# Seven block products for the r and z gates of a five-layer gated graph network, with two groups in flight, on one Trainium2 core

## The chip, the core and the metric

The kernel runs on one core of one Trainium2 chip. Time is device time in microseconds (us). Before any change it is 2644.72 us (median of 3 runs, 2644.05 to 2645.42). The *granted clock* is the share of TensorE's full clock that the profile records; 1.00 is full speed. The kernels are judged faster or slower when they differ by more than 2%.

Five engines work side by side: TensorE (PE in the profile, its weight loads PEld), VectorE (DVE), ScalarE (ACT), GpSimd (POOL) and SyncE (SP, which here only starts DMAs). The program gives each its own instructions in a fixed order.

## The reference

There are 128 graphs of 64 nodes with 256 features. The first stage runs five layers of message passing with a gated cell. Three other residual stages with a layer norm each follow. Only the first stage changes.

```python
def _gru_cell(m, h, w_ih, w_hh, b_ih, b_hh):
    gi = m @ w_ih.T + b_ih
    gh = h @ w_hh.T + b_hh
    i_r, i_z, i_n = jnp.split(gi, 3, axis=-1)
    h_r, h_z, h_n = jnp.split(gh, 3, axis=-1)
    r = jax.nn.sigmoid(i_r + h_r)
    z = jax.nn.sigmoid(i_z + h_z)
    n = jnp.tanh(i_n + r * h_n)
    return (1.0 - z) * n + z * h
...
for l in range(weight.shape[0]):                    # 5 layers
    m = jnp.einsum('bnd,de->bne', h, weight[l])
    agg = jnp.einsum('bij,bid->bjd', A, m)
    h = _gru_cell(agg, h, w_ih, w_hh, b_ih, b_hh)
...                                                 # then: layer norm, neighbour MLP, tangent-space
...                                                 # support, attention, each with a layer norm
```

## The kernel before

Eight graphs, 512 rows, make a group. There are 16 groups, and three are in flight (`NF = 3` sets of buffers). The program is written as one stream of operations per group. A helper, `Flow`, merges the streams into one order for each engine. It looks a few operations ahead (`AHEAD`) and works with durations written into the program. Everything of a layer lies transposed: 256 features as two tiles `c` of 128 partitions, and 512 rows along the free dimension.

A layer first turns the state into rows (`ps_hr`), then sums over neighbours (`ps_agg`). The message weights are multiplied into the gate weights once, at the start (`wmih`). Names that begin with `p_` or `ps_` are *banks*, the buffers that TensorE writes its results to. `hT` is the state, `x` the input of a group, `x_n` the result of a layer norm, and `junk_d` a scratch tile of the attention. What follows the five layers is called the *late stages*. For each of the two feature tiles:

```python
    AHEAD = {"PE": 24, "DVE": 6, "ACT": 6, "POOL": 4, "SP": 2}
    ...
    NF = 3
    ...
                wmi = wmih[l]
                i_n = 2 * KD + c
                p_r = gate(0, [(whhT, hT), (wmi, agg)], "p_r")      # 4 matmuls of 512 columns
                p_hn = gate(2, [(whhT, hT)], "p_hn")                # 2
                p_in = gate(2, [(wmi, agg)], "p_in")                # 2
                p_z = gate(1, [(whhT, hT), (wmi, agg)], "p_z")      # 4
                ...                                                 # r, n, and h - n on ACT and DVE
                act(512, lambda p=p_z, z=tb, c=c: nc.scalar.activation(
                    z.tile(), p.tile(), AF.Tanh, bias=half_b[:, KD + c:KD + c + 1], scale=0.5), [tb], [p_z, half_b])
                dve(512, lambda d=tc_, z=tb: nc.vector.scalar_tensor_tensor(
                    d.tile(), z.tile(), 1.0, d.tile(), OP.add, OP.mult), [tc_], [tc_, tb])
                dve(512, lambda d=tc_, t=ta, h=hn: nc.vector.scalar_tensor_tensor(
                    h.tile(), d.tile(), 0.5, t.tile(), OP.mult, OP.add), [hn], [tc_, ta])
```

The gate z comes last. So only a tanh and two VectorE steps lie between the last matmul and the new state.

Of the kernel before, what the change touches and what calls it, by code (L numbers as in the profile page):

```python
# [50 lines left out]
class Flow:  # L51
# [8 lines left out]
    AHEAD = {"PE": 24, "DVE": 6, "ACT": 6, "POOL": 4, "SP": 2}  # L60
# [83 lines left out]
def kernel(  # L144
# [28 lines left out]

    nc = tc.nc
# [11 lines left out]
    NF = 3  # L186
# [25 lines left out]
    def pe(n, run, w, r):  # L212
        flow.op("PE", {512: 0.86, 256: 0.46, 257: 0.46, 128: 0.33}.get(n, 0.3), run, w, r)
# [58 lines left out]
    whhT = [fixed([P, 3 * D], f"whhT{k}") for k in range(KD)]  # L272
    wattT = [fixed([P, D], f"wattT{k}") for k in range(KD)]


    wmih = [[fixed([P, 3 * D], f"wmih{l}_{k}") for k in range(KD)] for l in range(L)]
# [6 lines left out]
    vecs = fixed([NC, P], "vecs")  # L283
    nmr = fixed([NBLK, P], "nmr")
# [10 lines left out]
    for src, q, tag in ((w_hh, "sync", "hT"), (w_ih, "scalar", "half"), (att_w, "scalar", "agg")):  # L295
        nf = src.shape[0] // P
        for c in range(0, nf, 2):
            raw = {"hT": unit("hT", S, f"raw_hh{c}", (P, 2, D), 4),
                   "half": unit("ABC"[c // 2], S, f"raw_ih{c}", (P, 2, D)),
                   "agg": unit("agg", S, "raw_att", (P, 2, D), 2)}[tag]  # L300
            flow.op("SP" if q == "sync" else "ACT", 3.0 if q == "sync" else 0.1,
                    lambda raw=raw, src=src, c=c, q=q: getattr(nc, q).dma_start(
                        raw.tile(), src.rearrange("(c p) d -> p c d", p=P)[:, c:c + 2, :]), [raw])
            raw_of[src.tensor.name, c] = raw
    wms = []
    for l in range(L):
        wm = [unit("xn", S, f"wm{l}", (P, KD, D), 2), unit("xn", S, f"wm{l}", (P, KD, D), 2),
              unit("y", S, f"wm{l}", (P, KD, D)), unit("x", S, f"wm{l}", (P, KD, D)),
              unit("y", S - 1, f"wm{l}", (P, KD, D))][l]
        flow.op("ACT", 0.1, lambda wm=wm, l=l: nc.scalar.dma_start(  # L310
            wm.tile(), w_msg[l].rearrange("(k p) e -> p k e", p=P)), [wm])
        wms.append(wm)
# [15 lines left out]
    def turned(src, nf, dsts):  # L328
        for k in range(KD):
            for c0 in range(0, nf, 4):  # L330
                n = min(4, nf - c0)
                ps = bank("ps_w")
                for c in range(c0, c0 + n):
                    raw = raw_of[src.tensor.name, c - c % 2]
                    turn(lambda ps=ps, raw=raw, c=c, c0=c0, k=k: nc.tensor.transpose(
                        ps[:, (c - c0) * P:(c - c0 + 1) * P], raw[:, c % 2, k * P:(k + 1) * P], ident.tile()),
                        [ps], [raw, ident])
                dve(n * P, lambda ps=ps, k=k, c0=c0, n=n: nc.vector.tensor_copy(
                    dsts[k][:, c0 * P:(c0 + n) * P], ps[:, :n * P]), [(dsts[k], c0)], [ps])

    wihT = [unit("hr", S, f"wihT{k}", (P, 3 * D), 2) for k in range(KD)]
    turned(w_hh, 3 * KD, whhT)
    turned(w_ih, 3 * KD, wihT)

    for l in range(L):
        ps = bank("ps_wmT")
        for e in range(KD):
# [4 lines left out]
        wmT = unit("hT" if l % 2 else "agg", S, f"wmT{l}", (P, KD, D), 4 if l % 2 else 2)  # L352
        dve(512, lambda ps=ps, wmT=wmT: nc.vector.tensor_copy(
            wmT.tile(), ps.tile().rearrange("p (e d) -> p e d", d=D)), [wmT], [ps])
        for k in range(KD):
            for j, n in ((0, 2 * D), (2 * D, D)):
                ps = bank("ps_wmih")
                for e in range(KD):
                    pe(n, lambda ps=ps, wmT=wmT, e=e, k=k, j=j, n=n: matmul(
                        ps[:, :n], wmT[:, e, k * P:(k + 1) * P], wihT[e][:, j:j + n], e, KD),  # L360
                        [ps], [wmT, wihT[e]])
                act(n, lambda ps=ps, l=l, k=k, j=j, n=n: nc.scalar.copy(wmih[l][k][:, j:j + n], ps[:, :n]),
                    [(wmih[l][k], j)], [ps])
# [6 lines left out]
    turned(att_w, KD, wattT)  # L370
# [13 lines left out]
    def bih(i):  # L384
        return cols[:, i:i + 1]
# [10 lines left out]
    def group(g):  # L396
# [12 lines left out]
        def rows_T(tag, name, bufs, src):  # L409

            dst = [u(tag, f"{name}{k}", bufs=bufs) for k in range(KD)]
            for k in range(KD):
                ps = bank("ps_T")
                for b in range(NB):
                    turn(lambda ps=ps, b=b, k=k: nc.tensor.transpose(  # L415
                        ps[:, b * P:(b + 1) * P], src[:, b, k * P:(k + 1) * P], ident.tile()), [ps], [(src, b)])
                act(R, lambda ps=ps, k=k: nc.scalar.copy(dst[k].tile(), ps.tile()), [dst[k]], [ps])
            return dst
# [30 lines left out]
        hT = rows_T("hT", "hT", 4, xt)  # L449


        hr = None
        for l in range(L):
            agg = [u("agg", f"agg{l}_{c}", bufs=2) for c in range(KD)]
            for c in range(KD):
                if l:
                    hr = u("hr", f"hr{l}_{c}", (P, NB, P), 2)
                    ps = bank("ps_hr")
                    for b in range(NB):
                        turn(lambda ps=ps, b=b, h=hT[c]: nc.tensor.transpose(  # L460
                            ps[:, b * P:(b + 1) * P], h[:, b * P:(b + 1) * P], ident.tile()), [ps], [hT[c]])
                    act(512, lambda ps=ps, hr=hr: nc.scalar.copy(hr.tile(), tiles_of(ps.tile())), [hr], [ps])
                ps = bank("ps_agg")
                for b in range(NB):
                    def one(ps=ps, b=b, c=c, l=l, hr=hr):
                        h = hr[:, b, :] if l else xt[:, b, c * P:(c + 1) * P]
                        matmul(ps[:, b * P:(b + 1) * P], h, ed[:, b, :], 0, 1)
                    pe(128, one, [ps], [hr if l else xt, ed])
                act(512, lambda ps=ps, a=agg[c]: nc.scalar.copy(a.tile(), ps.tile()), [agg[c]], [ps])  # L469
            hN = [u("hT", f"hT{l}_{c}", bufs=4) for c in range(KD)]  # L470
            for c in range(KD):
                def gate(i, sides, name):
                    ps = bank(name)
                    f = slice((i * KD + c) * P, (i * KD + c + 1) * P)
                    n = len(sides) * KD
                    for a, (w, v) in enumerate(sides):
                        for k in range(KD):
                            pe(512, lambda a=a, k=k, w=w, v=v: matmul(ps.tile(), w[k][:, f], v[k].tile(), a * KD + k, n),
                               [ps], [w[k], v[k]])
                    return ps  # L480

                wmi = wmih[l]
                i_n = 2 * KD + c
                p_r = gate(0, [(whhT, hT), (wmi, agg)], "p_r")
# [272 lines left out]
```

## Time and profile before

| what | before |
|---|---|
| time, median | 2644.72 us |
| TensorE busy | 2563.2 us, 97% |
| VectorE, ScalarE, GpSimd busy | 50%, 35%, 12% |
| second to thirteenth output store | 1727.22 us, 157.0 a group |
| TensorE in that stretch | busy 1719.65 us, granted clock 1.00 |

The **period** is the time of the thirteenth output store less that of the second, divided by 11. It is the time that a group costs in the steady state. The view by windows splits it into TensorE's busy and idle time. Its columns are the window, its length, the busy time (and count) of PE, PEld, DVE, ACT and POOL, the granted clock, the DMA share and GB/s. For the kernel before:

```profile
452.96:2180.18 1727.22, 1719.65 (x5911) 969.18 (x5910) 890.65 (x2175) 630.65 (x1105) 215.32 (x242) 1.00 0.03 8
```

1719.65 of 1727.22: in a period of 157.0 us TensorE is busy for 156.3 and idle for 0.7. The largest wait of TensorE in this stretch, with its total, number and longest, is:

```profile
PE ps_hr L460 <- DVE hT L506: 2.8, 4, 1.0
```

### The profile page before, as it was taken

The page shows a single profiled execution, that of the slowest core. Times are in us where ns is not written, and L with a number is a line of the kernel's source. Part 1 is how long each engine was busy: PE and PEld are TensorE (multiplying, and loading weights), DVE is VectorE, ACT ScalarE, POOL GpSimd, SP SyncE. Part 2 cuts the span into 40 slices and gives each one's busy share as a digit, 9 for nine tenths or more (in the row PEclk, how much of TensorE's full clock was granted, in tenths as well). Part 3 has the DMA queues.
Part 4 walks back from the last instruction along what each step waited for, and adds up shares of the span by engine and source line. Part 5 has one row for each costly group of instructions (what it writes and reads, how often), then busy time and mean ns, then how long its engine had stood idle before and what let it go on. Part 6 is the DMA issues. An engine that isn't in the chain of part 4 may idle for free.

```text
span 2642.7 us, 24329 instructions
## 1 busy us (share of the span) xinstructions
PE 2563.2 (97%) x8770; PEld 1448.5 (55%) x8770; DVE 1312.2 (50%) x3191; ACT 933.4 (35%) x1637; POOL 321.5 (12%) x374
## 2 busy tenths in 40 slices
PE   6999999999999999999999999999999999999974
PEld 4556555464655556565565655546465564655543
DVE  1335455463555535455464555536455463545535
ACT  2334333342433334333343433334333333433321
POOL 1002010100202002020110202011020200202010
PEclk9999999999999999999999999999999999999986
DMA  4000000000000000000000000000000000000000
GB/s 120 3 0 10 9 3 17 0 11 8 3 16 3 16 0 11 9 3 16 3 9 8 11 8 3 17 0 11 8 1 16 1 8 9 1 9 1 8 0 8
DMA packets 30696, 26.24 MB, mean 10 GB/s; under 512 B 9668, under 2 KB 30176, under 8 KB 30576
## 3 DMA queue, kind: packets, MB, share of 16 engines
q1 hardware_dynamic: 26416, 19.67, 2.4%
q10 hardware_dynamic: 3760, 4.46, 0.6%
q8 instruction: 69, 1.13, 0.2%
q0 software_dynamic: 400, 0.57, 0.1%
q14 instruction: 51, 0.42, 0.1%
HBM read 16.30 MB, written 8.39 MB: 9 GB/s over the span
## 4 chain that ended last, share of the span: by engine, by line
PE 89%; DVE 5%; ACT 2%; POOL 1%; DMA 1%; issue 1%; POOLq 0%; DVEq 0%; SPq 0%; ACTq 0%
PE p_r L210 19%; PE p_z L210 19%; PE p_hn L210 10%; PE p_in L210 10%; PE ps_o L210 9%; PE ps_hid L210 8%; PE ps_agg L210 5%; PE ps_a L210 2%; PE ps_hr L460 2%; PE ps_wmih L210 1%; PE ps_T L415 1%; PE ps_att L210 1%; DVE st L424 1%; PE ps_sup L210 1%; POOL rstd L427 1%
## 5 line engine op out<-in xcount | busy, mean ns | idle before, releaser
L210 PE MATMUL p_r<-hT,whhT 128*128 128x512 f32 x640 | 311.8, 593 | 0.0
L210 PE MATMUL p_r<-agg,wmih 128*128 128x512 f32 x640 | 304.6, 593 | 0.9 <-ACT agg L469 0.9
L210 PE MATMUL p_hn<-hT,whhT 128*128 128x512 f32 x640 | 305.1, 592 | 0.0
L210 PE MATMUL p_in<-agg,wmih 128*128 128x512 f32 x640 | 304.9, 592 | 0.0
L210 PE MATMUL p_z<-agg,wmih 128*128 128x512 f32 x640 | 304.8, 593 | 0.0
L210 PE MATMUL p_z<-hT,whhT 128*128 128x512 f32 x640 | 304.4, 592 | 0.0
L495 DVE SCALAR_TENSOR_TENSOR A<-A,B 128x512 f32<-128x512 f32 x160 | 114.4, 715 | 360.0 <-ACT B L493 359.6
L498 ACT ACTIVATE A<-A,cols 128x512 f32<-128x512 f32 x160 | 115.5, 722 | 319.6 <-DVE A L497 319.6
L210 PE MATMUL ps_hid<-aggm,w1s 128*128 128x512 f32 x512 | 223.6, 595 | 0.2 <-ACT aggm L540 0.2
L491 ACT ACTIVATE A<-p_r,half_b 128x512 f32<-128x512 f32 x160 | 109.7, 686 | 313.8 <-PE p_r L210 252.9
L501 ACT ACTIVATE B<-p_z,half_b 128x512 f32<-128x512 f32 x160 | 109.6, 685 | 304.2 <-PE p_z L210 304.1
L426 POOL TENSOR_SCALAR ve<-mv 128x4 f32<-128x4 f32 x64 | 19.0, 297 | 1622.4 <-DVE mv L425 1622.4
L504 DVE SCALAR_TENSOR_TENSOR C<-B,C 128x512 f32<-128x512 f32 x160 | 113.9, 712 | 178.3 <-ACT B L501 175.3
L210 PEld LDWEIGHTS p_r<-agg,wmih 128*128 128x128 f32 x640 | 118.5, 190 | 136.5 <-issue 133.2
L210 PEld LDWEIGHTS p_z<-hT,whhT 128*128 128x128 f32 x640 | 119.6, 190 | 133.9 <-issue 130.6
L210 PEld LDWEIGHTS p_in<-agg,wmih 128*128 128x128 f32 x640 | 119.7, 190 | 133.5 <-issue 130.6
L210 PEld LDWEIGHTS p_hn<-hT,whhT 128*128 128x128 f32 x640 | 119.0, 190 | 132.2 <-issue 124.4
L210 PEld LDWEIGHTS p_z<-agg,wmih 128*128 128x128 f32 x640 | 119.6, 190 | 130.9 <-issue 129.6
L210 PE MATMUL ps_o<-w2s,hid 128*128 128x256 f32 x768 | 182.8, 384 | 5.1 <-DVE hid L587 5.1
L210 PEld LDWEIGHTS ps_o<-w2s,hid 128*128 128x128 f32 x768 | 146.9, 193 | 40.8 <-issue 9.1
L500 DVE TENSOR_TENSOR C<-hT,A 128x512 f32<-128x512 f32 x160 | 118.1, 738 | 97.0 <-ACT A L498 97.0
L210 PEld LDWEIGHTS p_r<-hT,whhT 128*128 128x128 f32 x640 | 112.6, 191 | 95.0 <-issue 91.1
(160 smaller groups left out, 3245.4 us busy)
## 6 DMA issues: line engine op xcount, KB each, us to landing
x<-in_x_dram SPq DMA_DIRECT2D x16, 512.0 KB, 3.9
out_dram<-x_n SPq DMA_DIRECT2D x16, 512.0 KB, 2.9
a_raw<-in_adj_dram SPq DMA_DIRECT2D x32, 64.0 KB, 2.5
wm<-in_L_gnn_weight_dram ACTq DMA_DIRECT2D x5, 256.0 KB, 7.0
w1s<-in_L_gnn_W_dram ACTq DMA_DIRECT2D x1, 1024.0 KB, 11.2
w2s<-in_L_gnn_W_dram ACTq DMA_DIRECT2D x1, 1024.0 KB, 11.2
raw_ih<-in_L_gnn_w_ih_dram ACTq DMA_DIRECT2D x3, 256.0 KB, 5.3
raw_hh<-in_L_gnn_w_hh_dram SPq DMA_DIRECT2D x3, 256.0 KB, 6.8
```

What stands on the lines that cost most here:

```text
L210: nc.tensor.matmul(o, lhsT, rhs, start=(k == 0), stop=(k == nk - 1))
L415: turn(lambda ps=ps, b=b, k=k: nc.tensor.transpose(ps[:, b * P:(b + 1) * P], src[:, b, k * P:(k + 1) * P], ident.tile()), [ps], [(src, b)])
L424: dve(256, lambda b=b: nc.vector.bn_stats(st[:, b, :], y[:, b, :]), [(st, b)], [(y, b)])
L426: pool(0.23, lambda: nc.gpsimd.tensor_scalar(ve.tile(), mv[:, :, 1], LN_EPS, None, OP.add), [ve], [mv])
L427: pool(1.04, lambda: nc.gpsimd.tensor_tensor(rstd.tile(), ve.tile(), m_half, OP.pow), [rstd], [ve])
L460: turn(lambda ps=ps, b=b, h=hT[c]: nc.tensor.transpose(ps[:, b * P:(b + 1) * P], h[:, b * P:(b + 1) * P], ident.tile()), [ps], [hT[c]])
L491: act(512, lambda p=p_r, t=ta, c=c: nc.scalar.activation(t.tile(), p.tile(), AF.Tanh, bias=half_b[:, c:c + 1], scale=0.5), [ta], [p_r, hal ...
L495: dve(512, lambda t=ta, v=tb: nc.vector.scalar_tensor_tensor(t.tile(), t.tile(), 1.0, v.tile(), OP.add, OP.mult), [ta], [ta, tb])
L498: act(512, lambda t=ta, i=i_n: nc.scalar.activation(t.tile(), t.tile(), AF.Tanh, bias=bih(i)), [ta], [ta, cols])
L500: dve(512, lambda d=tc_, h=hc, t=ta: nc.vector.tensor_sub(d.tile(), h.tile(), t.tile()), [tc_], [hc, ta])
L501: act(512, lambda p=p_z, z=tb, c=c: nc.scalar.activation(z.tile(), p.tile(), AF.Tanh, bias=half_b[:, KD + c:KD + c + 1], scale=0.5), [tb], ...
L504: dve(512, lambda d=tc_, z=tb: nc.vector.scalar_tensor_tensor(d.tile(), z.tile(), 1.0, d.tile(), OP.add, OP.mult), [tc_], [tc_, tb])
```

## The change

Gates r and z are a block product. The left factor is the 2 x 2 block matrix of a11, a12 (message and state weights of r) and a21, a22 (those of z). The right factor has the summed message `a` above the state `h`, each cut into row halves 0 and 1. Eight block products give it in the plain way. Strassen's method, in a form with few sums, needs seven. The weight sums s1 to s4 are made once on the chip. Four sums of data (t1 to t4) go to GpSimd in each layer. Five sums of products (`plus`) go to VectorE. TensorE should lose an eighth of its work on r and z. The five weight sets for each layer and the sums take so much on-chip memory that only two groups fit.

```diff
-    AHEAD = {"PE": 24, "DVE": 6, "ACT": 6, "POOL": 4, "SP": 2}
+    AHEAD = {"PE": 32, "DVE": 10, "ACT": 10, "POOL": 4, "SP": 2}
...
-    NF = 3
+    NF = 2
+    HR = R // 2
...
+            for o, x0, x1 in ((s1[l], a21, na22), (s2[l], s1[l], a11[l]), (s3[l], a11[l], a21), (s4[l], a12, s2[l])):
...
+        def product(ps, w, v, first, last, r):
+            for c in range(KD):
+                for k in range(KD):
+                    pe(256, lambda c=c, k=k: nc.tensor.matmul(
+                        ps[:, c * HR:(c + 1) * HR], w[:, k, c * P:(c + 1) * P], v(k), ...
...
+            minus(t1, of(a, 1), of(a, 0), [a])                       # GpSimd
+            minus(t2, of(h, 1), lambda: view(t1), [(h, 1), t1])
+            minus(t3, of(h, 1), of(a, 1), [(h, 1), (a, 1)])
+            minus(t4, lambda: view(t2), of(h, 0), [t2, (h, 0)])
+            ...                                                      # state part of n, as before
+            product(p1, a11[l], k_of(a, 0), True, False, (a, 0))
+            act(512, lambda: nc.scalar.copy(u1.tile(), blocks_of(p1.tile())), [u1], [p1])
+            product(p_in[0], w_in[l], k_of(a, 0), True, True, (a, 0))
+            product(p1, a12, k_of(h, 0), False, True, (h, 0))
+            tanh_half(ur, lambda c: p1[:, c * HR:(c + 1) * HR], 0, p1)   # r, half 0
+            product(pu, s2[l], k_view(t2), True, True, t2)
+            plus(uu, pu, u1)                                         # VectorE
+            product(pv, s3[l], k_view(t3), True, False, t3)
+            plus(uv, pv, uu)
+            product(p_in[1], w_in[l], k_of(a, 1), True, True, (a, 1))
+            product(pv, na22, k_view(t4), False, True, t4)
+            plus(uz, pv, uu)
+            tanh_half(uz, lambda c: uz[:, c, :], 1, uz)              # z, half 0
+            new_state(0, ur, uz)
+            product(pw, s1[l], k_view(t1), True, False, t1)
+            plus(uv, pw, uv)                                         # must read pw ...
+            product(pw, s4[l], k_of(h, 1), False, True, (h, 1))      # ... before this adds to it
+            plus(uu, pw, uu)
+            tanh_half(uu, lambda c: uu[:, c, :], 0, uu)              # r, half 1: the last
+            tanh_half(uv, lambda c: uv[:, c, :], 1, uv)              # z, half 1
+            new_state(1, uu, uv)
```

`new_state` is five VectorE steps of 512 and one tanh in two parts. It ends with the new state of that row half. In the profile of after, `ta` and `tb` are the tiles of t1 to t4, and U, V, Z, R are the gates and their partial sums.

## The prediction

> **What bounds the kernel now.** I read the busy shares and the slices first, then the chain, then the costliest groups, then the trace in order of time in three places: the steady state, the last group's last layer, and the last group's later stages.
>
> ```profile
> PE 2563.2 (97%) x8770; PEld 1448.5 (55%) x8770; DVE 1312.2 (50%) x3191; ACT 933.4 (35%) x1637; POOL 321.5 (12%) x374
> PE   6999999999999999999999999999999999999974
> PE 89%; DVE 5%; ACT 2%; POOL 1%; DMA 1%; issue 1%; POOLq 0%; DVEq 0%; SPq 0%; ACTq 0%
> L210 PE MATMUL p_r<-hT,whhT 128*128 128x512 f32 x640 | 311.8, 593 | 0.0
> L210 PE MATMUL ps_o<-w2s,hid 128*128 128x256 f32 x768 | 182.8, 384 | 5.1 <-DVE hid L587 5.1
> ```
>
> TensorE is full except at both ends: the busy table for 200 to 2400 us gives 198 to 200 us busy in every 200. So removed TensorE work is worth its whole length, as long as TensorE can still be kept fed. An fp32 matmul is two MATMUL records (640 for 320 matmuls). The 593 and 384 ns are latencies that overlap; the pitch comes from runs of one form in order of time:
>
> ```profile
> 1306.56 13.95 PE L210 MATMUL ps_hid<-aggm,w1s 128*128 128x512 f32 x32
> 1344.22 2.75 PE L210 MATMUL ps_o<-w2s,hid 128*128 128x256 f32 x12
> ```
>
> 512 columns: (13.95 - 0.593)/31 = 0.431 us a record, 0.86 a matmul. 256 columns: (2.75 - 0.38)/11 = 0.2155, so 0.431 a matmul. Half the columns cost exactly half: narrow products lose nothing here.
>
> The queue of output stores gives the rhythm: first store at 288.6, last at 2638.7. Group 14's attention matmuls begin at 2488.7, and a store follows them by 8.9 us (group 7: 1389.9 to 1398.8), so its store is near 2497.6. A group therefore costs (2497.6 - 288.6)/14 = 157.8 us, the last one alone adds 141, and 4 close the kernel.
>
> How tightly is one group chained? The last group runs alone from about 2492:
>
> ```profile
> 2515.10 1.88 PE L210 MATMUL p_z<-agg,wmih 128*128 128x512 f32 x4
> 2516.82 0.60 PE L460 MATMUL ps_hr<-ident,hT 128*128 128x128 f32 x4
> 2517.08 0.69 ACT L501 ACTIVATE B<-p_z,half_b 128x512 f32<-128x512 f32 x1 [2.05 <-PE p_z L210]
> 2517.80 0.69 DVE L504 SCALAR_TENSOR_TENSOR C<-B,C 128x512 f32<-128x512 f32 x1 [2.04 <-ACT B L501]
> 2518.53 0.69 DVE L506 SCALAR_TENSOR_TENSOR hT<-C,A 128x512 f32<-128x512 f32 x1
> 2519.29 0.64 PE L460 MATMUL ps_hr<-ident,hT 128*128 128x128 f32 x4
> ```
>
> After the last gate matmul only tanh and two VectorE steps stand before the new state: 2.47 us (2516.82 to 2519.29), half filled by transposes and aggregation of the other feature half. A layer takes 24.5 us (ps_hr at 2492.14 and 2516.82) for about 23.3 us of TensorE work. The other thing to feed around is the stages after the five layers:
>
> ```profile
> 2549.45 3.44 PE L210 MATMUL ps_agg<-edge,x_n 128*128 128x128 f32 x16 [5.08 <-DVE x_n L430]
> 2553.05 14.00 PE L210 MATMUL ps_hid<-aggm,w1s 128*128 128x512 f32 x32 [0.16 <-ACT aggm L540]
> 2569.83 1.84 PE L210 MATMUL ps_ss<-ones,sqs 128*128 128x1 f32 x8 [2.77 <-DVE sqs L562]
> 2576.95 8.47 PE L210 MATMUL ps_o<-w2s,hid 128*128 128x256 f32 x24 [2.83 <-DVE hid L587]
> 2603.97 3.46 PE L210 MATMUL ps_sup<-tan,adjT 128*128 128x256 f32 x8 [9.91 <-DVE tan L636]
> 2616.68 1.94 PE L415 MATMUL ps_T<-ident,x_n 128*128 128x128 f32 x8 [9.25 <-DVE x_n L430]
> ```
>
> About 90 us from the last layer to the attention, with some 40 us of TensorE work in it (two blocks of 14 us) and 50 us of waits, each 3 to 10 us, in which other groups must supply the matmuls.
>
> **What the Trainium skill says.** (1) "TensorE: Matmul & The Clock Gate", Step-by-step: weight loads are pulled ahead under running matmuls. Agrees: a load takes 190 ns, under the 215 ns pitch of 256 columns; the change nearly doubles the loads of a layer, and they stay hidden. (2) Same page, What's actually happening: after an idle window of about 3.4 us the clock falls to half. Agrees in the tail: granted clock 0.59 to 0.84 there, and the eight ps_sup records take 3.46 us, against 1.89 in full flow. So an idle gap of several us costs more than itself. (3) "SBUF — State Buffer", Who interferes with whom: a VectorE instruction with two SBUF inputs contends with a GpSimd instruction that reads SBUF. Agrees: the subtraction h - n is 692 ns in the median but 2473 at most, and the one at 1305.37 that took 2.47 us ran beside GpSimd's 2.36 us addition. The change gives GpSimd much more of this. (4) "PSUM — Partial Sum Buffer", The four PSUM rules: two column groups in one bank may share the first matmul's clearing flag; the product helper does this, so it should be correct; no run shows it yet.
>
> **The change, part by part** (per layer and group, 80 such).
> - TensorE, gates r and z: 16 matmuls of 512 (13.7 us) become 7 x 4 of 256 (28 x 0.431 = 12.1). Gain 1.72 us; 8.6 a group, 138 in all. The h part of n keeps 4 x 512; its message part, 4 x 512, becomes 8 x 256: the same time. Transposes and aggregations: as many as before. Pure work per group: 157.8 - 8.6 = 149.2.
> - VectorE: 10 steps of 512 become 15; 5 x 0.69 x 80 = +276 us, to about 1590 (60%). Not a bound.
> - ScalarE: 8 steps of 512 become 3 of 512 and 12 of 256 (about 0.47 us, from 0.42 to 0.50 us of other 256-wide steps): 5.6 to 7.6 us, +165, to about 1100 (42%).
> - GpSimd: four subtractions of 1.04 us, +333, to about 655 (25%). They start after aggregation, while TensorE has 9 us of products that don't need them (hn, two thirds of r1, n): hidden.
> - Setup: matmuls as before; 20 weight sums, four on VectorE for layer 0, the rest on GpSimd: a few us at the start.
> - The end of a layer gets longer. The last product gives r of the second half of the rows, and after it come: sum (0.69), tanh (0.9 in two), times (0.69), plus (0.66), tanh (0.9), h - n (0.66), times z (0.66), state (0.66), with 0.26 from TensorE: 6.1 us against 2.47. Then transposes, copy (0.58 + 0.25) and the second aggregation before hn may open its bank: about 0.9 more. In front of it, the S4 product waits 1 to 2 us until the sum of S1's has read the bank. About 8 us a layer without own TensorE work, less 0.9 of aggregation: 7 to 8, against 1.2 before. A lone layer: 21.6 + 8 = 29.6 us, longer than the 24.5 now, despite less work.
> - Two groups in flight, not three: the third can't fill. Group g + 2 has g's buffers and starts after g's attention.
>
> **What that costs.** While one group is in its late stages, the other fills its 50 us of waits with layers. It runs only in those waits, so its own gap of 8 us begins in one. Going through the list of waits, with gaps starting anywhere in them, the blocks of 14, 14, 3.5 and 1.8 us cover about a third: 5.4 us stay empty. At 21.6 us of work a layer, 50/(21.6 + 5.4) = 1.9 gaps: about 10 us a period. Where both are in layers, the second finishes about one layer in the first's gap: up to 3 more. Against it: interleaving in pieces of 0.43 to 0.86 us stretches both chains, so that more of a gap lies under the other's work. The trace of before with just two groups (2420 to 2490) loses about 2 us, with gaps of 1.2; that scales to 8 or so. I take 9.
>
> Period: 149.2 + 9 = 158.2. First store: 48 us to the first gate as now, five layers of 30 with setup matmuls in their gaps, 95 to the end of the late stages, about 10 of mutual delay: 303. After group 14's store: 141, as the longer layers make up for a little less of them. Sum: 303 + 14 x 158.2 + 141 + 4 = 2663. I shade it by 10 since the whole was evidently written (deeper lookahead, 256-column time corrected) to fill two groups well: 2653.
>
> **Rivals.** (a) TensorE stays full with two groups: extra idle 2 to 3 us a period, 448 + 14 x 152 = 2576, 2.6% faster. For it: 99.5% busy today, and late stages under one other group lose little; against it: today's gaps are a sixth as long. (b) The chain becomes the bound: 14 us of gaps a period and half clock after some of them, 448 + 14 x 164 = 2744. For it: the tail's halved clock and GpSimd blocking VectorE steps up to 2.47 us; against it: two groups of serial length near 5 x 29.6 + 97 = 245 need only 123 us a period. (c) VectorE as the bound: 1590 us busy speaks against it, except beside ps_o, where 11 us of its steps feed 14 us of matmuls. It would add a few us a period, inside (b). (d) Weight loads show: 190 under 215 ns leaves 25; if they did at 5 ns a record, 56 x 80 x 0.005 = 22 us.
>
> **Range and chances.** Break-even is 157 us a period, or 8 us of new idle, close to what I find; each us is 14 us of total. Idle of 2 to 14 gives 2560 to 2735. Under 4 us it is faster by 2%, above 11.7 slower by 2%. Chances 0.30, 0.42, 0.28.
>
> **What would show it.** Records of 256 at 0.2155 pitch; TensorE busy near 2425; busy share in the middle about 94%; waits of 4 to 7 us before ps_hr, named after the state on VectorE, where now they are under 1; stores 158 apart; VectorE near 1590. Spacing under 153 with no such waits would prove my gap costing wrong; a granted clock under 1.00 in mid-run would prove it too mild.

## The result, and the profile after

The changed kernel is correct and takes **3026.68 us** (median of 4 runs, 3022.21 to 3030.89), against 2644.66 of the kernel before in the same rounds. The ratio is 1.1444 (95% interval 1.1424 to 1.1464): slower by 14%, far outside the range. A ratio here is the mean time of one kernel's fast runs over that of the other's of the same rounds, so it is not quite the ratio of the medians quoted.

The page of the changed kernel: busy shares, the slices of TensorE and of its granted clock, the chain that ended last, and four of its groups (count, busy us, mean ns, then the idle time before and what ended it).

```profile
PE 2583.6 (86%) x11330; PEld 1986.3 (66%) x11330; DVE 1681.8 (56%) x3593; ACT 1082.5 (36%) x2211; POOL 763.9 (25%) x708
...
PE   7998989988898888979888898888988888898774
...
PEclk9999989999999999999999999999999999999887
...
PE 49%; DVE 25%; ACT 5%; POOL 3%; issue 3%; DMA 0%; POOLq 0%; DVEq 0%; ACTq 0%; SPq 0%
...
L531 POOL TENSOR_TENSOR ta<-agg 128x512 f32<-128x512 f32 x80 | 105.0, 1313 | 858.7 <-ACT agg L467 832.7
L473 PE MATMUL p_in<-agg,w_in 128*128 128x256 f32 x1280 | 307.0, 379 | 0.0
...
L473 PE MATMUL p_w<-hT,s 128*128 128x256 f32 x640 | 162.7, 397 | 76.6 <-DVE V L565 76.4
...
L454 PE MATMUL ps_hr<-ident,hT 128*128 128x128 f32 x640 | 107.1, 298 | 110.0 <-DVE hT L586 105.6
```

TensorE is no longer full: the slices are 8 where they were 9. The chain is TensorE for 49% of the span, where it was 89%, and VectorE for 25%, where it was 5%. So in a quarter of the span the step that set the end was one of VectorE's. The last two groups of the fence show the two places in the changed layer: the transposes that open a layer wait for the new state, and the last product of a layer waits for the sum that must read its bank first.

The windows view of the steady state (second to thirteenth store) of the changed kernel, same columns as before:

```profile
473.56:2481.17 2007.61, 1747.68 (x7738) 1349.91 (x7737) 1156.50 (x2455) 735.22 (x1498) 508.25 (x462) 0.96 0.02 7
```

The period is 2007.61 / 11 = 182.5 us, 25.5 more than before. TensorE is busy for 158.9 of them and idle for 23.6. It has less work and is yet busy for longer, above all because the granted clock is 0.96 here. An experiment below (e12) ran the seven products at clock 1.00, and there TensorE is busy for 150.7 us a period. So the period of 182.5 is 150.7 of work, 8.2 of longer busy time and 23.6 of idle. Of the 8.2, the clock records of the trace account for 5.8: half of the time that TensorE is busy while they show half clock. The other 2.4 are not clock. In e1 below, too, TensorE is busy for 1.6 us longer than in the kernel before, at a clock of 1.00, when the same work is broken by more waits.

What ended the idle time of TensorE in that stretch (total us, times, longest):

```profile
PE ps_hr L454 <- DVE hT L586: 65.1, 33, 4.0
PE p_w L473 <- DVE V L565: 54.8, 32, 3.5
PE ps_agg L213 <- DVE x_n L488: 41.5, 11, 4.0
PE ps_T L444 <- DMA x<-in_x_dram: 34.1, 10, 3.5
PE ps_e L785 <- DVE junk_d L780: 22.6, 11, 2.1
```

Three of the five are not in the changed layer at all. They are waits of the late stages and, in the fourth line, for the next group's input. The kernel before had these steps too, but other groups filled the waits. In order of time, TensorE looks so in one steady period of the changed kernel (start, length, then what; in brackets the idle time before it and what ended it):

```profile
1277.29 1.99 PE L473 MATMUL p_w<-hT,s 128*128 128x256 f32 x8 [0.95 <-DVE V L565]
...
1279.55 1.89 PE L473 MATMUL p_w<-ta,s 128*128 128x256 f32 x8
...
1282.59 1.99 PE L473 MATMUL p_w<-hT,s 128*128 128x256 f32 x8 [0.70 <-DVE V L565]
1287.33 1.06 PE L454 MATMUL ps_hr<-ident,hT 128*128 128x128 f32 x8 [2.74 <-DVE hT L586]
1292.37 3.78 PE L213 MATMUL ps_agg<-edge,x_n 128*128 128x128 f32 x16 [3.98 <-DVE x_n L488]
...
1349.37 1.99 PE L473 MATMUL p_w<-hT,s 128*128 128x256 f32 x8 [3.42 <-DVE V L565]
```

Between 1277 and 1284 the last products of a layer of both groups stand close together: both groups come to the end of a layer at once. After 1284.6 neither has a matmul that may run, so 2.74 and then 3.98 us stay empty. The 16 records of `ps_agg` then take 3.78 us where they take 1.95 in full flow, which is half clock.

### The profile page after: what moved, and what is told of

Read it like the earlier page. It is cut to its first block, busy times and chain, and to the rows that moved or that the text cites. A ratio compares the mean times of both kernels' runs of the same rounds, so it can differ in the third digit from the quotient of the medians.

```text
span 3020.4 us, 31201 instructions
## 1 busy us (share of the span) xinstructions
PE 2583.6 (86%) x11330; PEld 1986.3 (66%) x11330; DVE 1681.8 (56%) x3593; ACT 1082.5 (36%) x2211; POOL 763.9 (25%) x708
## 4 chain that ended last, share of the span: by engine, by line
PE 49%; DVE 25%; ACT 5%; POOL 3%; issue 3%; DMA 0%; POOLq 0%; DVEq 0%; ACTq 0%; SPq 0%
PE ps_o L213 7%; PE ps_hid L213 6%; PE p_hn L213 5%; PE p_r L473 5%; PE p_v L473 5%; PE ps_agg L213 5%; PE p_in L473 4%; PE p_w L473 4%; DVE junk_d L780 3%; PE p_u L473 3%; DVE d L584 3%; DVE st L482 2%; POOL rstd L485 2%; PE ps_hr L454 2%; DVE hT L586 2%
## 5 line engine op out<-in xcount | busy, mean ns | idle before, releaser
L213 PE MATMUL p_hn<-hT,w_hn 128*128 128x512 f32 x640 | 326.8, 636 | 0.0
L473 PE MATMUL p_in<-agg,w_in 128*128 128x256 f32 x1280 | 307.0, 379 | 0.0
L473 PEld LDWEIGHTS p_in<-agg,w_in 128*128 128x128 f32 x1280 | 241.9, 190 | 32.6 <-issue 0.5
L473 PE MATMUL p_w<-hT,s 128*128 128x256 f32 x640 | 162.7, 397 | 76.6 <-DVE V L565 76.4
L213 PE MATMUL ps_hid<-agg,w1s 128*128 128x512 f32 x512 | 225.0, 598 | 0.8 <-ACT agg L467 0.8
L581 ACT ACTIVATE t<-t,cols 128x256 f32<-128x256 f32 x320 | 146.2, 500 | 204.6 <-DVE t L579 203.0
L454 PE MATMUL ps_hr<-ident,hT 128*128 128x128 f32 x640 | 107.1, 298 | 110.0 <-DVE hT L586 105.6
L213 PEld LDWEIGHTS ps_agg<-edge,hr 128*128 128x128 f32 x1024 | 142.0, 199 | 50.8 <-ACT hr L518 36.2
L213 PE MATMUL ps_agg<-edge,hr 128*128 128x128 f32 x1024 | 156.9, 286 | 11.5 <-ACT hr L518 11.4
L473 PE MATMUL p_r<-hT,a 128*128 128x256 f32 x640 | 163.3, 381 | 2.4 <-ACT s L590 2.4
L473 PE MATMUL p_u<-ta,s 128*128 128x256 f32 x640 | 160.2, 380 | 0.0
```

The source lines that it names most:

```text
L213: nc.tensor.matmul(o, lhsT, rhs, start=(k == 0), stop=(k == nk - 1))
L454: turn(lambda j=j, c=c: nc.tensor.transpose(ps[:, j * D + c * P:j * D + (c + 1) * P], src[:, c, (2 * n + j) * P:(2 * n + j + 1) * P], iden ...
L473: pe(256, lambda c=c, k=k: nc.tensor.matmul(ps[:, c * HR:(c + 1) * HR], w[:, k, c * P:(c + 1) * P], v(k), start=first and c == k == 0, sto ...
L581: act(256, lambda c=c: nc.scalar.activation(t[:, c, :], t[:, c, :], AF.Tanh, bias=bih(2 * KD + c)), [(t, c)], [(t, c), cols])
```

## The experiments

Fourteen kernels ran, each with one profile and one timed round beside the kernel before (2644.1 to 2644.9 us). The table has the medians, the ratios, and the periods with their split. "Work" in the text means TensorE busy time.

| run | us | ratio | period | busy + idle | clock |
|---|---|---|---|---|---|
| before | 2644.7 | 1 | 157.0 | 156.3 + 0.7 | 1.00 |
| after | 3026.7 | 1.144 | 182.5 | 158.9 + 23.6 | 0.96 |
| e1 before, two groups | 2685.7 | 1.016 | 160.1 | 157.9 + 2.2 | 1.00 |
| e6 eight products | 2689.6 | 1.017 | 160.7 | 158.4 + 2.3 | 1.00 |
| e10 eight, r last | 2804.7 | 1.061 | 166.9 | 160.6 + 6.3 | 0.99 |
| e11 eight, idle subtractions | 2768.4 | 1.047 | 166.0 | 160.5 + 5.5 | 0.99 |
| e16 eight, r last, idle sums | 2965.7 | 1.121 | 177.5 | 164.9 + 12.6 | 0.97 |
| e17 eight, all parts | 3070.2 | 1.161 | 184.4 | 167.7 + 16.7 | 0.95 |
| e4 seven, no subtractions (wrong) | 2945.9 | 1.114 | 178.0 | 161.3 + 16.8 | 0.93 |
| e8 r and z swapped | 3022.5 | 1.143 | 181.8 | 159.1 + 22.8 | 0.96 |
| e9 input tile of its own | 3060.9 | 1.157 | 184.9 | 161.2 + 23.7 | 0.94 |
| e14 stalls filled | 2883.5 | 1.090 | 173.4 | 155.9 + 17.5 | 0.98 |
| e15 = e9 and e14 | 2925.0 | 1.106 | 176.8 | 156.0 + 20.8 | 0.96 |
| e18 = e14, no subtractions (wrong) | 2795.9 | 1.057 | 168.0 | 155.3 + 12.7 | 0.98 |
| e2 seven, three groups (wrong) | 2757.2 | 1.043 | 163.5 | 153.6 + 9.9 | 0.98 |
| e12 = e2, no subtractions (wrong) | 2609.8 | 0.987 | 154.5 | 150.7 + 3.8 | 1.00 |

"Wrong" marks kernels that compute a wrong result, with the same instructions in number and size except for the part named. All others are correct.

### Is it the loss of the third group alone?

**e1** takes the kernel before and gives it two groups.

```diff
-    NF = 3
+    NF = 2
```

> The kernel before with two sets of group buffers instead of three, nothing else. The period between output stores (second to thirteenth) was 157.0 us before and 182.5 us after. Theory A (two groups alone are the loss, whatever the gates): nearly all of it appears here, period 180 or more, about 2950 us. Theory B (two groups hurt because the new layers end in a long chain): the old layer leaves gaps of only 1.2 us, so period 160 to 166, 2690 to 2770 us, the loss being mostly the late input load and the half clock. Theory C (GpSimd's subtractions and VectorE's extra sums lengthen every chain): period at most 163.

Measured: 2685.68 us, period 160.1. Two groups cost the old layer 3.1 us a period of the 25.5. The theory that two groups are simply too few falls for the old layer.

**e6** keeps the layout of the change (row halves, products of 256 columns, two groups, the deeper lookahead). It computes r and z by eight plain products, r before z. There are no weight sums, no subtractions and no sums of products.

```diff
-    ... seven products, five plus(...), four minus(...)
+            def gate(ps, wa, wh, n):
+                product(ps, wa, k_of(a, n), True, False, (a, n))
+                product(ps, wh, k_of(h, n), False, True, (h, n))
+            for n in range(2):
+                gate(pr, a11[l], a12, n)         # then tanh
+                product(p_in[n], w_in[l], k_of(a, n), True, True, (a, n))
+                gate(pz, a21[l], a22, n)         # then tanh
+                new_state(n, r_, z_)
```

> The changed kernel's layout with row halves and two groups, but with the plain eight block products: no weight sums, no subtractions, no sums after the products (the result must be right). TensorE work is back to 157 us a group, and after the last product only tanh of z and two VectorE steps follow, as before. Theory A: period still 180 or more, above 3000 us. Theory B: gaps of 2 to 3 us a layer, period 161 to 168, 2700 to 2800 us: with more multiplications faster than the changed kernel. Theory C: the same as B, so this run only tells A from the others.

Measured: 2689.56 us, period 160.7. Layout, narrow products and lookahead cost 0.6 us a period. So everything else of the loss comes with the seven products and what belongs to them.

**e2** gives the seven products a third group. For room, all layers share two weight tiles for the message weights and their sums, so the result is wrong, and the setup is about 30 us shorter.

```diff
-    NF = 2
+    NF = 3
-    a11, s1, s2, s3, s4, w_in = ([gate_w(f"{n}_{l}") for l in range(L)] for n in (...))
+    a11, s1 = ([gate_w(f"{n}_{l}") for l in range(1)] * L for n in ("a11", "s1"))
+    s2, s3, s4, w_in = s1, s1, s1, a11
```

> The changed kernel with three sets of group buffers. They only fit because one small set of weights serves all layers and all sums, so the result is wrong on purpose; the instructions of a group are the same, the setup is some 30 us shorter. Theory A and B: a third group fills the gaps, period 149 to 154 us, 2480 to 2540 us in all. Theory C: chains stay long but are filled too unless an engine is full; period 160 or more, about 2650 us.

Measured: 2757.18 us, period 163.5, that is 19.0 less than with two groups. The new layer needs a third group, which the old one hardly does. But even with three groups, and less work, it is slower than the kernel before. So there is a loss besides the missing group. This stretch of its trace (all engines, in order of time) shows one part of it:

```profile
1303.97 1.75 DVE L589 SCALAR_TENSOR_TENSOR hT<-d,t 128x512 f32<-128x512 f32 x1
...
1305.14 1.70 POOL L534 TENSOR_TENSOR tb<-hT,agg 128x512 f32<-128x512 f32 x1
1305.65 1.74 DVE L587 SCALAR_TENSOR_TENSOR d<-V,d 128x512 f32<-128x512 f32 x1
1306.81 1.70 POOL L534 TENSOR_TENSOR ta<-hT,ta 128x512 f32<-128x512 f32 x1
1307.43 1.63 DVE L589 SCALAR_TENSOR_TENSOR hT<-d,t 128x512 f32<-128x512 f32 x1
...
1309.12 1.11 PE L457 MATMUL ps_hr<-ident,hT 128*128 128x128 f32 x4 [4.90 <-DVE hT L589]
```

VectorE and GpSimd take turns. Steps of VectorE that take 0.69 us elsewhere take 1.63 to 1.75, and the subtractions of GpSimd 1.70 instead of 1.27 (their median in e11 below, where VectorE's steps are not slowed). Three such steps stand one behind the other in VectorE's queue (the first ends one group's layer, the other two end another's), and TensorE waits 4.90 us for the last.

### What do the four subtractions cost?

**e4** takes the subtractions out of the changed kernel. The products read plain row halves instead.

```diff
-            minus(t1, ...); minus(t2, ...); minus(t3, ...); minus(t4, ...)
-            product(pu, s2[l], k_view(t2), True, True, t2)
+            product(pu, s2[l], k_of(h, 1), True, True, (h, 1))
...                                       # pv, pv second part and pw in the same way
```

> The changed kernel without the four GpSimd subtractions of a layer (the products read the halves of h and of the aggregate directly; wrong result on purpose), two groups. Theory C: most of the loss goes, period about 165, 2770 us. Theories A and B: only the contention with VectorE goes, a few us; period 176 to 181, 2930 to 3000 us.

Measured: 2945.87 us, period 178.0, so 4.5 us a period. The idle time fell by 6.8, but the granted clock fell too, from 0.96 to 0.93, which took 2.4 back. **e12** does the same to e2, with three groups.

> The seven products with three groups and one set of weights, as in the run with period 163.5 us and 2757 us, now without the subtractions (wrong on purpose twice over). Contention theory: the chains are back to their own length and three groups fill them: period 150 to 154, 2540 to 2590 us. Gap theory: the chain at the layer's end stays and with it most of the loss: 158 to 163, 2660 to 2750 us.

Measured: 2609.75 us, period 154.5: 9.0 us less than e2, and 2.5 less than the kernel before. Its windows line is the one that gives the full-clock work of the seven products, 1657.98 / 11 = 150.7:

```profile
443.58:2142.92 1699.34, 1657.98 (x7698) 1300.13 (x7697) 1046.11 (x2455) 722.42 (x1498) 222.60 (x242) 1.00 0.03 8
```

With a third group and no subtractions TensorE is nearly full again, and the saved work shows. But this kernel is wrong, and its setup is shorter, so its 1.3% is no usable gain.

**e11** puts the four subtractions into e6, unread.

```diff
+            minus(t1, of(a, 1), of(a, 0), [a])           # and t2, t3, t4; nothing reads them
```

> The eight plain products on two groups, plus the four GpSimd subtractions of each layer, whose results nothing reads: the chain is unchanged, only GpSimd is busy as in the changed kernel. Gap theory: period 161 to 163. Contention theory: VectorE's two-input steps stretch from 0.69 to 0.8 to 1.2 us and the period goes to 168 or more, above 2800 us.

Measured: 2768.42 us, period 166.0: 5.3 us a period for work that nobody waits for. This lies between the two expectations, and neither gave the reason. In this kernel it is not contention. The VectorE steps at the end of a layer keep their length (690 ns for `hT<-d,t` in both). A group's late stages, however, have small steps on GpSimd, and these now stand behind the subtractions of the other group. VectorE's wait for one of them, a small power step ahead of the tangent-space support, in e6 and then in e11 (total us, times, longest):

```profile
DVE n L677 <- POOL n L676: 42.1, 16, 2.7
```

```profile
DVE n L684 <- POOL n L683: 95.1, 16, 6.2
```

That is (95.1 - 42.1) / 16 = 3.3 us more a group in the chain of the late stages, at this one wait. Another power step later in the chain gives some of it back (54.6 to 26.8 us in all). That the queue is the reason shows on GpSimd itself: in e6 it waited for the input of the first of these steps 16 times, 48.1 us in all, and in e11 once, 2.7 us. It was still at the subtractions when the input came.

### What does the later end of a layer cost?

**e10** is e6 with z before r, so that r comes last as in the change. Nothing is added.

```diff
-    r, in, z
+    z, in, r          # per row half; new_state as before
```

> The eight plain products on two groups (period 160.7 us, 2690 us), with the order of the gates turned round so that r is the last product of a half: the chain behind it grows by about 3.3 us (two sums and a tanh more after the last product), no sums and no subtractions. Gap theory: period 166 to 172, 2770 to 2860 us. Contention theory: at most 163, 2720 us.

Measured: 2804.66 us, period 166.9: 6.2 us a period for the order alone. Little of it is a wait for the new state (8.6 us in the steady state, see e16). TensorE stands for the next group's input `x` and for `x_n` instead, 30.6 and 26.4 us: so a longer chain can show at other places than its own end. One of these waits, of 2.82 us, in order of time:

```profile
598.14 1.92 PE L438 MATMUL ps_T<-ident,x 128*128 128x128 f32 x8 [2.82 <-DMA x<-in_x_dram]
```

One difference remains: e10 puts r last in both row halves, while in the change r of half 0 comes early.

**e8** tries the opposite on the changed kernel: it swaps the columns of r and z in the weights, so that z of half 1 comes last.

```diff
-            new_state(0, ur, uz)
+            new_state(0, uz, ur)
-            new_state(1, uu, uv)
+            new_state(1, uv, uu)          # and the weight slices and biases to match
```

> The changed kernel with the two gates swapped in the block products, so that the last product gives z of the second half and r comes one product earlier: after it only a sum, tanh of z and two VectorE steps follow, some 3.2 us shorter a layer; same instructions, right result. Gap theory (the empty time is the chain at the layer's end, felt since only two groups run): period from 182.5 to about 170 us, 2830 us in all. Contention theory (GpSimd and VectorE block each other on two-input steps): only what the shorter chain saves in its share, period 177 to 181, about 2960 us.

Measured: 3022.5 us, period 181.8. It gains nothing. The wait of the last product for the sum is gone from the list of TensorE's waits, and the wait for the new state falls a little, from 65.1 to 57.5 us in the steady state. But others grow, such as that of the transposes for `x_n`, from 9.9 to 36.2. The swap makes r of half 0 late as well, so the VectorE steps of both halves fall at the end of the layer. That this is why is my reading, and no run tests it.

### What do the five sums cost on VectorE?

**e16** is e10 with five sums a layer on VectorE, from the same kind of bank, which nothing reads: one after each z, one after each r, and a second one after r of half 1.

```diff
+            def idle_sum(ps):
+                junk = u("U", f"idle_{l}", (P, KD, HR))
+                dve(512, lambda: nc.vector.tensor_add(junk.tile(), blocks_of(ps.tile()), ...), [junk], [ps, wb_r])
```

> The eight plain products on two groups with r last (period 166.9 us, 2805 us), plus five VectorE additions from PSUM in each layer that nothing reads: VectorE is loaded as in the changed kernel, GpSimd is not. If VectorE's load (more steps waiting in its queue) is what lengthens the chains: period 172 or more, 2890 us. If only the length of the chain counts: 167 to 169, 2810 to 2840 us.

Measured: 2965.7 us, period 177.5: 10.6 us a period. A period has 25 such sums of 0.687 us, so 17.2 us of VectorE work, on an engine that is 53% busy. TensorE's wait for the new state, in the steady state of e10 and then of e16:

```profile
PE ps_hr L448 <- DVE hT L570: 8.6, 14, 1.0
```

```profile
PE ps_hr L448 <- DVE hT L570: 61.5, 66, 1.9
```

It grew from 14 waits to 66. Of the 10.6 us, 6.3 are new idle time and 4.3 are longer busy time. By the clock records of the two traces, half clock during busy time grew from 2.1 to 4.9 us a period, so 2.8 of the 4.3 are clock. The sums after r stand in VectorE's queue while the tanh of r runs, so a part of the cost is a longer chain, as in the change itself. The sums also hold the banks of r and z for longer, but the list of TensorE's waits has none for such a bank. A rival stays: the added steps make `Flow` merge the streams in another order. Set side by side, TensorE's matmul groups stand in the same order to 92% in e10 and e16 (99% in e6 and e11, over 99% in e16 and e17). So the 10.6 us may in part be the order.

### Do the parts add up?

**e17** is e16 with the four unread subtractions: everything of the new layer except the seven products and the waits between them.

```diff
+            minus(t1, of(a, 1), of(a, 0), [a])           # and t2, t3, t4; nothing reads them
```

> The run with eight products, r last and five unread sums a layer on VectorE, plus the four unread subtractions on GpSimd: everything of the new layer but the seven products themselves and their waits in between. If the parts simply add (theory), the period is that run's 177.5 plus the 4.5 to 5.3 us that the subtractions cost in the two other pairs of runs: 182 to 183, about 3035 us in all, so as slow as the seven products although 8.6 us more of matmuls are in it. If they share one gap (rival), so that a later layer end hides the contention, it stays at 178 to 180 and near 2985 us; then the sum that I set up from single parts closes by luck.

Measured: 3070.16 us, period 184.4. The parts add, and a little more: the subtractions cost 6.9 here. This correct kernel with eight plain products is 1.4% slower than the seven products are, which is inside the 2%. Now there is contention too. In e16, and then in e17, the groups of two VectorE steps read:

```profile
L568 DVE SCALAR_TENSOR_TENSOR d<-Z,d 128x512 f32<-128x512 f32 x160 | 140.6, 879 | 3.5
...
L764 DVE SCALAR_TENSOR_TENSOR junk_d<-ho,a_r 128x256 f32<-128x256 f32 x128 | 54.1, 423 | 3.9
```

```profile
L575 DVE SCALAR_TENSOR_TENSOR d<-Z,d 128x512 f32<-128x512 f32 x160 | 155.7, 973 | 3.5
...
L771 DVE SCALAR_TENSOR_TENSOR junk_d<-ho,a_r 128x256 f32<-128x256 f32 x128 | 110.5, 863 | 3.9
```

The steps of the attention (`junk_d`) take twice as long, 863 ns instead of 423.

### The waits between the seven products

**e14** keeps the seven products and moves other matmuls of the same group into their waits: the state part of n (`hn`) and the message part (`p_in`).

```diff
-            p_hn; p1 first; p_in[0]; p1 second; pu; pv first; p_in[1]; pv second; pw first; pw second
+            hn(0); p1 first; hn(1); p1 second; pu; pv first; p_in[0]; pv second; pw first; p_in[1]; pw second
```

> The changed kernel with the same instructions of a layer in another order: one half of the hn product stands behind the first part of r1, the first half of n between the two parts of v, the second half of n between S1's and S4's products, so that no product waits for the reading of its own bank. If these waits (5.0 us a period before p_w) are a cost of their own: period 174 to 178, about 2920 us. If they are part of the same gap as the layer's end: 180 to 183.

Measured: 2883.54 us, period 173.4: 9.1 us a period gained, and correct. The wait of the last product for the sum fell from 76.4 us in the whole trace to 17.6, and the wait for the new state from 105.6 to 71.4.

**e9** gives the next group's input a tile of its own, so that its load need not wait for the last reader of a shared tile. That was to remove the wait for the DMA of x (34.1 us in the steady state).

```diff
-        xt = unit("x", s, f"x_{g}", (P, NB, D))
+        xt = unit("xt", s, f"x_{g}", (P, NB, D))     # and r in another tag, to make room
```

> The changed kernel with a tile of its own for the input rows, so that the next group's load no longer waits for the second late stage (room made by small scratch tiles sharing other tiles; ring waits put on every part of a buffer). If the load is a cost of its own, its 3.1 us a period of empty TensorE and the half clock behind it go: period 176 to 179, 2930 to 2970 us. If the load only stands at the head of a queue that had nothing else to do, the empty time moves to another waiter: period 181 to 183, same time within 20 us.

Measured: 3060.88 us, period 184.9. The wait for x is gone from the list, and it became no faster: the wait for the new state rose from 105.6 to 152.5 us in the whole trace. So the DMA had only stood first in TensorE's queue; behind it the same two groups had nothing to run. That is how I read it, with one reserve: to make room, the edit also lets scratch tiles share other tiles and adds waits for buffers, and these may have cost what the early load gained. **e15** is e9 and e14 together.

> Both together. If both are costs of their own the gains add, period 170 to 175, about 2840 us. If the chain at the layer's end on two groups is the cause, the period stays above 176. Either way slower than the kernel before.

Measured: 2925.0 us, period 176.8, which is slower than e14 alone. The early input, with what it needs, doesn't help here either.

**e18** takes the subtractions out of e14.

> Seven products on two groups in the order of the run with the stalls filled, without the four subtractions (the products read plain halves, so the result is wrong on purpose). If contention and the waits between the products add (theory), the period is 173.4 less 4.5 to 5.3: 168 to 169, about 2810 us; still 11 above the 157 of the kernel before, which then belongs to the five sums and r at the end on two groups. If the subtractions cost only by making those waits longer (rival), nothing is left to gain from both: 172 to 173 and near 2875 us.

Measured: 2795.94 us, period 168.0, 5.4 us less than e14. It also closes the account from the other side. It has the late end of the layer and the five sums, as e16 has, but seven products for eight. In full-clock work eight take 158.4 us a period (e6) and seven 150.7 (e12), a difference of 7.7; and 177.5 - 7.7 = 169.8 comes near the measured 168.0.

No run on two groups beats the kernel before. The nearest to it that keeps the layout is e6, 1.7% slower, which by the 2% counts as the same.

## Why the prediction was wrong

**What held.** The narrow products cost half of the wide ones: in a row of eight records (the one at 1279.55 above) seven pitches take 1.89 less the 0.38 of one record, 1.51 us, 0.216 each, against the predicted 0.2155, and e6 shows no loss from them. The removed work was predicted as 8.6 us a group and measured as 7.7 (158.4 to 150.7). Weight loads stayed hidden. ScalarE came out at 1082 us (predicted 1100), GpSimd at 764 (655) and VectorE at 1682 (1590). VectorE's is longer because GpSimd blocks some of its steps. Most of GpSimd's excess is a mis-sized cost: a subtraction takes 1.27 us in the median of e11, and never under 1.25, for the 1.04 of the prediction; 320 times the difference is 74. Why it is longer than other GpSimd steps of this size (1.04) no run shows. The rest is blocking. The kernel is correct, so the shared clearing flag of its point (4) works. The waits before the opening transposes are named after the state on VectorE, as foretold, but they are 2.0 us on average and 4.0 at most in the steady state, for 4 to 7. So the mechanism, a longer layer end that two groups can't cover, is there, but it is only a part: these waits are 5.9 of the 23.6 us of idle time a period, the last product's wait 5.0, and the three largest of the late stages and the input 8.9. TensorE is busy for 2584 us, not 2425, and for 87% of the steady state, not 94%. (One sum is slightly off, and nothing hangs on it: 2492.14 to 2516.82 is 24.7, not 24.5.)

**The step that failed** is "I take 9", for the idle time a period, and the overlap behind it: that the other group would cover all but 9 us of five layer ends of 8, and that nothing else would open. The measured idle time is 23.6. The busy time is 158.9 for the 149.2 of the prediction, and 5.8 of that is half clock. Together the period is 182.5 instead of 158.2. From the first to the fifteenth store the profile of after takes 180.8 a group (315.7 to 2846.6; the first of the 14 is only 157.9), and 14 times the 22.6 too much is 316 of the 374 us by which the prediction missed. The first store (315.7 for 303) adds 13, the shading of 10 the wrong way adds 10, and what follows the fifteenth store is 31 longer than the 145 of the prediction. (The profiled run is 4 us below the median.) Rival (b), the chain as the bound with 164 a period, pointed the right way but was too small by 18.5.

The experiments split the 25.5 us from 157.0 to 182.5, one addition after another:

| step | period | added |
|---|---|---|
| before, three groups | 157.0 | |
| two groups (e1) | 160.1 | 3.1 |
| row halves, 256 columns, lookahead (e6) | 160.7 | 0.6 |
| r at the end of the layer (e10) | 166.9 | 6.2 |
| five sums on VectorE (e16) | 177.5 | 10.6 |
| four subtractions on GpSimd (e17) | 184.4 | 6.9 |
| seven products for eight, and the waits between them (after) | 182.5 | -1.9 |

The last line is the whole purpose of the change. It removed 7.7 us of work and put waits in its place: 182.5 - (184.4 - 7.7) = 5.8 by this order, 9.1 by e14.

Point by point:

- **"Not a bound", of VectorE at 60%.** This was the largest error. Five sums a layer, unread in e16, take 17.2 us of an engine that is half idle, and cost 10.6 us a period. VectorE takes its steps in order, and each step of the layer's end stands behind whatever step of the other group came first. The prediction added the sums to a busy share and to the chain once. It did not add them to the wait of every other step in the queue. The wait that grew in e16, 8.6 to 61.5 us before the opening transposes, fits this; how much of it is the changed merging is not shown.
- **"Hidden", of the subtractions.** They were off the path to their own products, as said: no wait of TensorE in the list above names GpSimd. But they cost 4.5 to 6.9 us a period with two groups. e11 shows delayed small steps of the late stages in GpSimd's queue. e2 and e17 show VectorE and GpSimd blocking each other in turn, which "SBUF — State Buffer", Who interferes with whom, in the Trainium skill describes. The prediction cited that very section, saw a subtraction of 2473 ns in the trace of before, and put it into rival (b) only.
- **"1 to 2 us" for the last product's wait.** It was counted into the gap of 8 us at the end of a layer, to be covered with it. It is a second place in each layer where TensorE stands, 54.8 us in the steady state. Filling the waits from the same group (e14) gains 9.1.
- **The clock.** The prediction said that a clock below 1.00 in mid-run "would prove it too mild", and had no term for it. The clock records put 5.8 us a period on it. Half clock follows waits and makes each idle us dearer, as "TensorE: Matmul & The Clock Gate", HAM oscillation, in the Trainium skill describes: from e10 to e16 the step of 6.3 us of idle time came with 2.8 us of clock.
- **"Cover about a third".** The estimate let each gap start anywhere in the other group's late stages, whose matmuls were to cover a third of it, and let a layer of the other group cover nearly all of it otherwise. In the trace both groups end a layer together once in nearly every period (1277 to 1284 us above; 10 times in the steady state the last products of the two start 5.3 us apart, and the other layer ends stand 11 us or more apart, most of them 30 to 67). And the waits on `x_n`, on x and on `junk_d`, 98 us in the steady state, stay empty too. Why the two groups fall into this order I did not settle. The program merges the streams with durations written into it, such as 1.04 us for a subtraction that takes 1.31 to 1.40 on average in after, so its order may be off. No run tested that. Each experiment changes this order along with what it is meant to change, as said at e16.

**Left open.** The additions are measured in one order, and with two groups they are not quite independent: the subtractions cost 4.5, 5.3, 5.4 and 6.9 in four pairs of runs. The five sums' cost in e16 is that of unread sums. Two of these fall beside a tanh on the chain of r, so the split into a longer chain and a fuller queue is not separated. A third group for the correct seven products was not tried, as it does not fit into the memory.

## What to carry to other kernels

When a change removes work from a full engine but puts steps on the others, ask how many groups of work are in flight to cover the new waits, and price each added step by the queue that it stands in, not by the busy share of its engine. A half-idle engine that works in order can cost more than half of every step added to it: in e16 it was 0.6 us for each us added. Build the cheap counterparts first: the old arithmetic in the new layout, then with the new steps added unread, tells in a few runs which part costs what.

## What the Trainium skill lacked or had wrong

- "TensorE: Matmul & The Clock Gate", What's actually happening and HAM oscillation: the idle window of about 3.4 us fits the trace of after (half clock behind waits of 2.74 and 3.98 us). But its rule, no idle gaps over about 3.4 us, is too mild here, and a section on frequent short idle spells gives no length for them. In e16 no wait of TensorE listed in the steady state is over 2.9 us, and yet the granted clock there is 0.97, with 0.83 in the 20 us from 1160. In e10 the single wait of 2.82 us shown there is enough: in the 8 us before the clock falls no other is over 0.3 us, and the 3.4 us from 598.2 run at clock 0.50. Transposes stand behind this wait, so what the window counts as idle is not settled.
- No page gives the time of an fp32 matmul; "FP8 and Floating Point Precision" only counts its passes. Here an fp32 matmul is two records of 0.431 us each for 512 columns (0.2155 for 256).
- "SBUF — State Buffer", Who interferes with whom: agrees that a VectorE step with two SBUF inputs and a GpSimd step that reads SBUF contend. Its figures, 6.8 times slower for VectorE and 1.5 for GpSimd, come from opposite issue orders. It has none for two engines that take turns: in e2, 0.69 us steps of VectorE became 1.63 to 1.75, and subtractions of GpSimd of 1.27 us (median of e11) became 1.70.
- "GPSIMD Engine Reference", 3.1 Elementwise, gives the cost of a two-input step by itself. No page says what such steps cost the small steps queued behind them: four unread subtractions a layer cost 5.3 us a period in e11 without lengthening the VectorE steps.
